# Edge attention on a graph: the scans of a step read PSUM in place, and k and q of a turn share one PSUM tile of two banks

## The chip, the cores and the metric

The kernel runs on one core of a Trainium2 chip. The metric is the time of one execution in device microseconds; several runs give a median. A profile is taken of one more execution.

## The reference

A pre-norm attention layer on a graph of 12,500 nodes with 128 features and 212,500 edges, 8 heads of 16. The edges come sorted by destination, and every node has an edge to itself.

```python
h = jnp.maximum(_layernorm(x, axis=-1), 0.0)
# in the layer, node_h is h
q = (node_h @ Wq.T + bq).reshape(N, NUM_HEADS, HEAD_DIM)
k = (edge_h @ Wk.T + bk).reshape(-1, NUM_HEADS, HEAD_DIM)
v = (node_h @ Wv.T + bv).reshape(N, NUM_HEADS, HEAD_DIM)
qs, qd = (q[src], q[dst])
in_m = jnp.sum(qs * k, axis=-1)
out_m = jnp.sum(qd * k, axis=-1)
diag_m = jnp.sum(qs * qd, axis=-1)
score = (_segment_softmax(in_m * SCALE, dst, N) + _segment_softmax(out_m * SCALE, dst, N)
         + _segment_softmax(diag_m * SCALE, dst, N)) * att
h = jax.ops.segment_sum(score[..., None] * v[dst], dst, num_segments=N)
out = h @ Wo.T + bo        # reshaped to 128 features; then leaky_relu, and x is added
```

Every edge thus needs three products of 128 features (q of its source, q of its destination, k of the edge), summed by head to 24 logits. Each of the 24 columns goes through a softmax over the edges of one destination; its maximum over a destination's run of edges is found with scans.

## The kernel before

There are two paths in the file; with edges sorted by destination `ordered_path` runs. A head part makes the table of q for all nodes in memory (`q_table`). Then comes the loop that takes most of the time: 83 steps t (G = 83) of 5 turns s (S = 5), g = 5t + s, 415 turns in all. A turn is 512 edges, as 4 groups of 128 (BE = 512, JN = 4). A tail brings the last steps and the output of the last nodes.

The order on every engine is written out by hand: `pin` ties each instruction to the one before it on its engine. Engines wait for each other by semaphores that the framework puts in from the tiles that instructions share. Each turn issues, in this order:

- `turn(g+2)`: TensorE transposes the edge features (4 transposes into `eT_ps`, one PSUM bank), ScalarE copies them to `eT`.
- `spread_q(g+1)`: 4 matmuls of a one-hot matrix with a window of q rows (`win`) bring q of the destinations into `qd_ps`; ScalarE copies it to `qd` (L1268), because VectorE needs it also as the partner of k, which lies in PSUM.
- `project(g+1)`: a bias matmul (L1255) and 8 matmul records of fp32 (L1257) make k in `k_ps`.
- `logits(g)`: VectorE multiplies q of the sources with q of the destinations (L1276), with k (L1277), and `qd` with k (L1278), then sums by head (L1279).
- `one_hots(g+3)`: ScalarE makes the one-hot matrix of a later turn (L698, L699).

POOL (GpSimd) gathers q of the sources, 4 indirect DMAs a turn, 26 turns ahead (L707). Each is made to wait for a product instruction of TensorE, so that it is issued close behind it: the first for the transposes of the turn, the second for the q matmuls, the third for the k matmuls, the fourth for the last one of the turn:

```python
turn(g + 2);     behind[g + 1, 0] = pinned[products]
spread_q(g + 1); behind[g + 1, 1] = pinned[products]
project(g + 1);  behind[g + 1, 2] = pinned[products]
...
behind[g + 1, 3] = pinned[products]
```

Beside this, each step does once what the softmax of two steps earlier needs. At s = 4, `turn_logits(t-1)` transposes the logits to 120 rows (5 turns x 24 columns) by 512 edges, `l_ps`, and at s = 0 `turn_head(t-1)` transposes the first 64 edges of them, `h_ps`: a run of edges may go on into the next block, so a scan needs up to 64 logits beyond its end. ScalarE copies both into one tile `u` of 576 (L1304, L1318). At s = 1, `scan_both(t-2)` makes a forward and a backward maximum scan over the 576 with `far` (0 within a run, far below between runs). At s = 2, `turn_max` transposes the maxima to `m_ps`, and `powers` subtracts (VectorE, L1389) and takes the exponential (ScalarE, L1390). At s = 3, `show_ends` makes a matrix that selects the window of destinations (`d_ps`, then ScalarE L1425, L1426), and `weigh_powers` multiplies with the edge weights (L1408). At s = 4, `to_rows` sums into rows of destinations (`w_ps`, L1436; ScalarE L1441), which `put_rows` sends to memory. Output nodes are made in between (`nodes_before`, `nodes_between`). The small PSUM tiles of these steps share three buffers.

Of the kernel before, what the change touches and what calls it, by code (L numbers as in the profile page):

```python
# [7 lines left out]
F32 = mybir.dt.float32  # L8
BF = mybir.dt.bfloat16
I32 = mybir.dt.int32  # L10
AF = mybir.ActivationFunctionType
ALU = mybir.AluOpType
# [9 lines left out]
FAR = 1e30  # L22
# [450 lines left out]
def ordered_path(ctx: ExitStack, tc: tile.TileContext, flag, x, src, dst, edge_attr, edge_weight,  # L473
# [19 lines left out]
    nc = tc.nc  # L493
# [7 lines left out]
    S = 5  # L501
# [149 lines left out]
    def fetch(t):  # L651
# [5 lines left out]
        if t < G:  # L657
            relb = load.tile([K3, S, BE], BF, name="relb")
            pin(nc.sync.dma_start(relb, rel_d[part].rearrange("(s b) e -> s b e", b=G)
                                  [None, :, at, :].to_broadcast([K3, S, BE])))  # L660
        n = (BE + HEAD if t < G - 2 else BE) + 1
        far = load.tile([R, BE + HEAD + 1], BF, name="far", bufs=4)
        lo = t * BE
        of = bass.AP(far_d.tensor, far_d.offset + lo, [[G * BE, S], [0, H3], [1, n]])
        pin(nc.sync.dma_start(far[:, :n], of))
        to = [mybir.EngineType.SP] if t < G else [mybir.EngineType.SP, mybir.EngineType.Activation]
# [573 lines left out]
    with tc.tile_pool(name="work", bufs=2) as work, \  # L1240
            tc.tile_pool(name="scan", bufs=2) as scan, \
            tc.tile_pool(name="ps", bufs=1, space=PSUM) as ps:
        ks, eTs, qds, q_ps, lTs = {}, {}, {}, {}, {}

        def turn(g):
            eT_ps = ps.tile([P, JN, P], F32, name="eT_ps", bufs=1)
            for j in range(JN):
                pin(nc.tensor.transpose(eT_ps[:, j, :], eas[g][:, j * F:(j + 1) * F], ident))  # L1248
            eT = work.tile([P, JN, P], F32, name="eT", bufs=2)
            pin(nc.scalar.copy(eT, eT_ps))  # L1250
            eTs[g] = eT

        def project(g):
            k_ps = ks[g] = ps.tile([P, JN, F], F32, name="k_ps", bufs=2)
            pin(nc.tensor.matmul(k_ps, ones3, bk3, start=True, stop=False))  # L1255
            for j in range(JN):
                pin(nc.tensor.matmul(k_ps[:, j, :], eTs[g][:, j, :], wk, start=False,  # L1257
                                     stop=(j == JN - 1)))
            del eTs[g]

        def spread_q(g):
            s, d = g % S, st[g // S]
            qd_ps = q_ps[g] = ps.tile([P, JN, F], F32, name="qd_ps", bufs=2)
            for j in range(JN):
# [6 lines left out]
        def logits(g):  # L1271
            s, t = g % S, g // S
            if s == 0:
                lTs[t] = scan.tile([P, JN, S, H3], F32, name="lT", bufs=4)
            prod = work.tile([P, JN, 3, F], F32, name="prod", bufs=1)
            pin(nc.vector.tensor_mul(prod[:, :, 1, :], qqs[g], q_ps[g]))  # L1276
            pin(nc.vector.tensor_mul(prod[:, :, 0, :], qqs[g], ks[g]))  # L1277
            pin(nc.vector.tensor_mul(prod[:, :, 2, :], qds[g], ks[g]))  # L1278
            pin(nc.vector.tensor_reduce(lTs[t][:, :, s, :],  # L1279
                                        prod.rearrange("p j i (h d) -> p j (i h) d", d=DIM), AX.X,  # L1280
                                        ALU.add))
            del ks[g], qds[g], q_ps[g], qqs[g]

# [12 lines left out]
        def turn_logits(t):  # L1296
            l_ps = small([R, P, JN], "l_ps")
            for j in range(JN):
                pin(nc.tensor.transpose(l_ps[:, :, j], lTs[t][:, j].rearrange("p s c -> p (s c)"),  # L1299
                                        ident))  # L1300
            l = st[t]["l"] = l_ps.rearrange("r p j -> r (p j)")
            if t < G - 2:
                u = st[t]["u"] = scan.tile([R, BE + HEAD], F32, name="u")
                pin(nc.scalar.copy(u[:, :BE], l))  # L1304

        def turn_head(t):
            n = HEAD // JN
            h_ps = small([R, n, JN], "h_ps")
            for j in range(JN):
                pin(nc.tensor.transpose(h_ps[:, :, j], lTs[t][:n, j].rearrange("p s c -> p (s c)"),  # L1310
                                        ident[:n, :n]))
            head = h_ps.rearrange("r p j -> r (p j)")
            if t == 0:
                l_few = scan.tile([R, HEAD], F32, name="l_few", bufs=1)
                pin(nc.scalar.copy(l_few, head))
                pin(nc.sync.dma_start(l_end[:R - H3, :], l_few[H3:, :]))
            else:
                pin(nc.scalar.copy(st[t - 1]["u"][:, BE:], head))  # L1318

# [20 lines left out]

        def scan_both(t):
            d = st[t]
            u, far = d["u"], d["far"]
            pin(nc.vector.tensor_tensor_scan(u, far[:, :BE + HEAD], u, last.get("u", -FAR), op0=ALU.add,
                                             op1=ALU.max))
            last["u"] = u[:, BE - 1:BE]
            m = d["m"] = scan.tile([R, BE + HEAD], F32, name="m")
            pin(nc.vector.tensor_tensor_scan(m[:, ::-1], far[:, BE + HEAD:0:-1], u[:, ::-1], -FAR,
                                             op0=ALU.add, op1=ALU.max))
# [14 lines left out]
        def scan_back(t):  # L1364
            d = st[t]
            if t < G:
                m = d["m"] = scan.tile([R, BE + HEAD], F32, name="m")[:, :BE]
                pin(nc.vector.tensor_tensor_scan(m[:, ::-1], d["far"][:, BE:0:-1], d["u"][:, ::-1],
# [94 lines left out]
        def later(f, t, *more):  # L1463
            if 0 <= t < T:
                f(t, *more)
# [217 lines left out]
        for g in range(end):  # L1683
# [17 lines left out]
            if s == 0:  # L1701
                later(turn_head, t - 1)
                later(select, t - 2)
            elif s == 1:
                later(scan_both, t - 2)
                if t == 3:
                    logits_few()
# [83 lines left out]
        for r, of in enumerate(rest):  # L1791
# [3 lines left out]
            halves_of(ab, engine)  # L1795
        names = ("eT_ps", "k_ps", "qd_ps", "qd_ps", "k_ps")
        for r in range(len(rest) + 2):
            if r < len(rest):
# [4 lines left out]
                of.turn(small([P, JN, P], "node_ps"))  # L1803
                of.project_o(ps.tile([P, JN, F], F32, name=names[r], bufs=1 if r == 0 else 2))
            if 0 <= r - 2:
# [47 lines left out]
```

## Time and profile before

| | |
|---|---|
| median of 3 runs | 2729.59 us (2725.22 to 2730.32) |
| profiled execution | 2736.8 us, span 2735.0 us |
| mean granted TensorE clock | 0.741 |
| TensorE busy | 1955.8 us (72%) |
| VectorE busy | 2035.8 us (74%) |
| ScalarE busy | 1455.5 us (53%) |
| GpSimd busy | 1610.2 us (59%) |
| memory read, written | 322.07 MB, 32.17 MB |

Busy time is that of an engine's own instructions; register, branch, semaphore and DMA-issuing instructions don't count. "PE" is TensorE's matmuls, "PEld" its weight loads, DVE is VectorE, ACT ScalarE, POOL GpSimd, SP the engine that issues most DMAs. In a row of the timeline the columns are the start, the duration, engine, line, operation, tiles and shapes, the number of equal instructions run together, and in brackets the idle time of the engine before it with what ended it; "remote" is a semaphore whose sender the view doesn't name. In a row of a group "| a, b | c" are busy time in all, mean of one in ns, and idle time in front of them.

### The profile page before, as it was taken

What the parts mean: (1) busy time and instruction counts of PE and PEld (TensorE: products, weight loads), DVE (VectorE), ACT (ScalarE), POOL (GpSimd) and SP (SyncE); (2) the same over time, 40 slices, a digit from 0 to 9 for tenths busy, and PEclk for the clock granted to TensorE, in tenths of its full rate; (3) what the DMA queues carried; (4) which work ended last, traced back from release to release, by engine and by line L of the source; (5) the groups of instructions that cost most, each with busy time, mean ns of one, the idle gap of its engine ahead of it and who ended that gap; (6) DMA issues with size and microseconds to landing.
All of it is one profiled execution on the core that took longest, in us unless ns stands there. A gap on an engine that the chain in (4) does not pass through costs nothing.

```text
span 2735.0 us, 37777 instructions
## 1 busy us (share of the span) xinstructions
PE 1955.8 (72%) x10956; PEld 1537.5 (56%) x10956; DVE 2035.8 (74%) x2644; ACT 1455.5 (53%) x2824; POOL 1610.2 (59%) x1683
## 2 busy tenths in 40 slices
PE   2366776776677777777777877777768777777886
PEld 1245665555555555555555655565556566555664
DVE  2265777777778777787777777787777777777995
ACT  1355765555555555555555555555555555555672
POOL 7516566666666666666666666666666666666100
PEclk9977777667777777776677677667777676768785
DMA  6256344554554455444444444444444544554431
GB/s 177 76 166 190 111 130 121 142 145 124 136 145 130 139 147 138 139 136 137 128 129 140 123 130 131 134 120 131 134 127 120 139 135 122 134 134 123 123 85 51
DMA packets 378949, 356.98 MB, mean 131 GB/s; under 512 B 192899, under 2 KB 298638, under 8 KB 378528
## 3 DMA queue, kind: packets, MB, share of 16 engines
q1 hardware_dynamic: 310109, 239.36, 30.4%
q0 software_dynamic: 53184, 108.92, 15.5%
q10 hardware_dynamic: 15440, 6.20, 0.9%
q8 instruction: 90, 1.47, 0.2%
q14 instruction: 126, 1.02, 0.1%
HBM read 322.07 MB, written 32.17 MB: 130 GB/s over the span
## 4 chain that ended last, share of the span: by engine, by line
PE 52%; issue 13%; ACT 13%; DVE 10%; another core or an unknown queue 9%; DMA 1%; SPq 0%; POOL 0%; ACTq 0%; DVEq 0%; POOLq 0%
PE k_ps L1257 14%; PE eT_ps L1248 8%; PE w_ps L1436 7%; PE qd_ps L1265 5%; PE k_ps L1255 4%; PE node_ps L1187 2%; PE m_ps L1380 2%; DVE lT L1279 2%; PE d_ps L1422 2%; ACT qd L1268 2%; ACT relb L698 2%; ACT eT L1250 2%; PE l_ps L1299 2%; ACT oh L699 1%
## 5 line engine op out<-in xcount | busy, mean ns | idle before, releaser
L707 POOL DMA_INDIRECT qq<-q_table,sources x1564 | 1503.5, 961 | 893.7 <-issue 339.7
L1279 DVE TENSOR_REDUCE lT<-prod 128x96 f32<-128x1536 f32 x415 | 727.5, 1753 | 14.3
L1257 PE MATMUL k_ps<-wk,eT 128*128 128x128 f32 x3320 | 637.6, 349 | 19.2 <-issue 18.4
L1257 PEld LDWEIGHTS k_ps<-wk,eT 128*128 128x128 f32 x3320 | 539.0, 246 | 156.9 <-issue 155.7
L1248 PE MATMUL eT_ps<-ident,ea 128*128 128x128 f32 x1660 | 352.4, 349 | 272.9 <-issue 161.7
L1248 PEld LDWEIGHTS eT_ps<-ident,ea 128*128 128x128 f32 x1660 | 249.1, 179 | 356.5 <-issue 210.3
L1276 DVE TENSOR_TENSOR prod<-qq,qd_ps 128x512 f32<-128x512 f32 x412 | 280.3, 680 | 192.1 <-ACT qd L1268 98.4
L1277 DVE TENSOR_TENSOR prod<-qq,k_ps 128x512 f32<-128x512 f32 x412 | 280.7, 681 | 185.6 <-remote 100.7
L1268 ACT COPY qd<-qd_ps 128x512 f32<-128x512 f32 x415 | 245.7, 592 | 254.4 <-PE qd_ps L1265 96.2
L1250 ACT COPY eT<-eT_ps 128x512 f32<-128x512 f32 x415 | 241.5, 582 | 253.5 <-remote 105.6
L1436 PE MATMUL w_ps<-back,sel 128*126 128x144 f32 (+1 forms) x1296 | 223.4, 347 | 122.7 <-ACT sel L1426 103.1
L698 ACT ACTIVATE relb<-relb,before 126x512 bf16<-126x512 bf16 x415 | 303.9, 732 | 0.0
L1436 PEld LDWEIGHTS w_ps<-back,sel 128*126 128x126 f32 (+1 forms) x1296 | 213.0, 241 | 134.1 <-ACT sel L1426 111.7
L1278 DVE TENSOR_TENSOR prod<-qd,k_ps 128x512 f32<-128x512 f32 x415 | 281.8, 679 | 0.0
L699 ACT ACTIVATE oh<-relb 126x512 bf16<-126x512 bf16 x415 | 261.3, 630 | 13.2
L1265 PE MATMUL qd_ps<-win,oh 126*128 126x128 bf16 x1660 | 209.6, 261 | 13.0 <-issue 12.8
L1255 PE MATMUL k_ps<-b,ones 3*128 3x512 bf16 x415 | 198.4, 478 | 4.1 <-issue 2.4
L1265 PEld LDWEIGHTS <-oh 126*128 126x128 bf16 x1660 | 167.8, 122 | 28.2 <-issue 13.3
L1390 ACT ACTIVATE back<-back 128x480 f32<-128x480 f32 x83 | 50.0, 603 | 186.4 <-DVE back L1389 119.4
L1380 PE MATMUL m_ps<-ident,m 120*128 120x120 f32 x332 | 72.1, 347 | 97.9 <-issue 70.5
L1389 DVE TENSOR_TENSOR back<-lT,m_ps 128x480 f32<-128x480 f32 x83 | 54.0, 650 | 112.6 <-PE d_ps L1422 71.6
L1425 ACT ACTIVATE sel<-d_ps 128x420 f32<-128x420 f32 x168 | 77.8, 512 | 94.4 <-remote 84.5
(232 smaller groups left out, 1955.8 us busy)
## 6 DMA issues: line engine op xcount, KB each, us to landing
ea<-in_edge_attr_dram SPq DMA_DIRECT2D x415, 256.0 KB
relb<-rel_d SPq DMA_DIRECT2D x83, 630.0 KB
qq<-q_table,sources POOLq DMA_INDIRECT x1564
win<-q_table SPq DMA_DIRECT2D x415, 31.5 KB
far<-far_d SPq DMA_DIRECT2D x81, 135.2 KB
q_table<-q SPq DMA_DIRECT2D x24, 384.0 KB
sums<-rows SPq DMA_DIRECT2D x411, 7.9 KB
q_table<-xq SPq DMA_DIRECT2D x24, 256.0 KB
```

Source lines behind the costliest of these rows:

```text
L698: pin(nc.scalar.activation(d, d, AF.Abs, bias=before[:K3]))
L699: pin(nc.scalar.activation(oh, d, AF.Relu, bias=1.0, scale=-1.0))
L707: rows = pin(nc.gpsimd.indirect_dma_start(out=qq[:, j, :], out_offset=None, in_=x if g < RAW else q_table, in_offset=bass.IndirectOffsetOn ...
L1248: pin(nc.tensor.transpose(eT_ps[:, j, :], eas[g][:, j * F:(j + 1) * F], ident))
L1250: pin(nc.scalar.copy(eT, eT_ps))
L1255: pin(nc.tensor.matmul(k_ps, ones3, bk3, start=True, stop=False))
L1257: pin(nc.tensor.matmul(k_ps[:, j, :], eTs[g][:, j, :], wk, start=False, stop=(j == JN - 1)))
L1265: pin(nc.tensor.matmul(qd_ps[:, j, :], ohs[g][:, j * P:(j + 1) * P], d["win"][:, s, :], start=(j == 0), stop=(j == JN - 1)))
L1268: pin(nc.scalar.copy(qds[g], qd_ps))
L1278: pin(nc.vector.tensor_mul(prod[:, :, 2, :], qds[g], ks[g]))
L1279: pin(nc.vector.tensor_reduce(lTs[t][:, :, s, :], prod.rearrange("p j i (h d) -> p j (i h) d", d=DIM), AX.X, ALU.add))
L1436: pin(nc.tensor.matmul(w_ps[:(hi - lo) * W, lo:hi].rearrange("p s c -> p (s c)"), d["sel"][:n, j, lo:hi, :].rearrange("p s w -> p (s w)"), ...
```

## The change

k and q of a turn get one PSUM tile of two banks, `qk_ps`. The products of q of the sources with q of the destinations and with k become one VectorE instruction of 128x1024; the product of `qd` with k stays. The tile `eT` gets a third buffer. ScalarE's copies into `u` are dropped: the forward scan of a step runs in place in `l_ps` at s = 0 (`scan_here`), and copies its last column to a carry tile of 120x1; the 64 columns beyond the end have two scans of their own, one forward from `h_ps` and one backward (`scan_head`, at s = 0), and the backward scan over the 512 starts from their result (`scan_back`, which the tail had, at s = 1). `far` is 513 wide instead of 577. `logits_few`, which runs once, moves from t = 3 to t = 1, and the end of the kernel takes its PSUM tiles from the new ones. Lines shift by up to 9.

```diff
--- before.py
+++ after.py
@@ -658,11 +658,10 @@
             relb = load.tile([K3, S, BE], BF, name="relb")
             pin(nc.sync.dma_start(relb, rel_d[part].rearrange("(s b) e -> s b e", b=G)
                                   [None, :, at, :].to_broadcast([K3, S, BE])))
-        n = (BE + HEAD if t < G - 2 else BE) + 1
-        far = load.tile([R, BE + HEAD + 1], BF, name="far", bufs=4)
+        far = load.tile([R, BE + 1], BF, name="far", bufs=4)
         lo = t * BE
-        of = bass.AP(far_d.tensor, far_d.offset + lo, [[G * BE, S], [0, H3], [1, n]])
-        pin(nc.sync.dma_start(far[:, :n], of))
+        of = bass.AP(far_d.tensor, far_d.offset + lo, [[G * BE, S], [0, H3], [1, BE + 1]])
+        pin(nc.sync.dma_start(far, of))
         to = [mybir.EngineType.SP] if t < G else [mybir.EngineType.SP, mybir.EngineType.Activation]
         loads, base_v[t] = nc.values_load_multi_w_load_instructions(
             places[0:1, t, 0:S], engines=to, min_val=0, max_val=N - 1,
@@ -1240,18 +1239,18 @@
     with tc.tile_pool(name="work", bufs=2) as work, \
             tc.tile_pool(name="scan", bufs=2) as scan, \
             tc.tile_pool(name="ps", bufs=1, space=PSUM) as ps:
-        ks, eTs, qds, q_ps, lTs = {}, {}, {}, {}, {}
+        qks, eTs, qds, lTs = {}, {}, {}, {}
 
         def turn(g):
             eT_ps = ps.tile([P, JN, P], F32, name="eT_ps", bufs=1)
             for j in range(JN):
                 pin(nc.tensor.transpose(eT_ps[:, j, :], eas[g][:, j * F:(j + 1) * F], ident))
-            eT = work.tile([P, JN, P], F32, name="eT", bufs=2)
+            eT = work.tile([P, JN, P], F32, name="eT", bufs=3)
             pin(nc.scalar.copy(eT, eT_ps))
             eTs[g] = eT
 
         def project(g):
-            k_ps = ks[g] = ps.tile([P, JN, F], F32, name="k_ps", bufs=2)
+            k_ps = qks[g][:, 0]
             pin(nc.tensor.matmul(k_ps, ones3, bk3, start=True, stop=False))
             for j in range(JN):
                 pin(nc.tensor.matmul(k_ps[:, j, :], eTs[g][:, j, :], wk, start=False,
@@ -1260,7 +1259,8 @@
 
         def spread_q(g):
             s, d = g % S, st[g // S]
-            qd_ps = q_ps[g] = ps.tile([P, JN, F], F32, name="qd_ps", bufs=2)
+            qks[g] = ps.tile([P, 2, JN, F], F32, name="qk_ps", bufs=2)
+            qd_ps = qks[g][:, 1]
             for j in range(JN):
                 pin(nc.tensor.matmul(qd_ps[:, j, :], ohs[g][:, j * P:(j + 1) * P],
                                      d["win"][:, s, :], start=(j == 0), stop=(j == JN - 1)))
@@ -1273,13 +1273,13 @@
             if s == 0:
                 lTs[t] = scan.tile([P, JN, S, H3], F32, name="lT", bufs=4)
             prod = work.tile([P, JN, 3, F], F32, name="prod", bufs=1)
-            pin(nc.vector.tensor_mul(prod[:, :, 1, :], qqs[g], q_ps[g]))
-            pin(nc.vector.tensor_mul(prod[:, :, 0, :], qqs[g], ks[g]))
-            pin(nc.vector.tensor_mul(prod[:, :, 2, :], qds[g], ks[g]))
+            pin(nc.vector.tensor_mul(prod[:, :, 0:2, :].rearrange("p j i f -> p i j f"),
+                                     qqs[g][:, None].to_broadcast([P, 2, JN, F]), qks[g]))
+            pin(nc.vector.tensor_mul(prod[:, :, 2, :], qds[g], qks[g][:, 0]))
             pin(nc.vector.tensor_reduce(lTs[t][:, :, s, :],
                                         prod.rearrange("p j i (h d) -> p j (i h) d", d=DIM), AX.X,
                                         ALU.add))
-            del ks[g], qds[g], q_ps[g], qqs[g]
+            del qks[g], qds[g], qqs[g]
 
         last = {}
         assert len(rest) <= REST
@@ -1298,10 +1298,7 @@
             for j in range(JN):
                 pin(nc.tensor.transpose(l_ps[:, :, j], lTs[t][:, j].rearrange("p s c -> p (s c)"),
                                         ident))
-            l = st[t]["l"] = l_ps.rearrange("r p j -> r (p j)")
-            if t < G - 2:
-                u = st[t]["u"] = scan.tile([R, BE + HEAD], F32, name="u")
-                pin(nc.scalar.copy(u[:, :BE], l))
+            st[t]["l"] = l_ps.rearrange("r p j -> r (p j)")
 
         def turn_head(t):
             n = HEAD // JN
@@ -1309,13 +1306,11 @@
             for j in range(JN):
                 pin(nc.tensor.transpose(h_ps[:, :, j], lTs[t][:n, j].rearrange("p s c -> p (s c)"),
                                         ident[:n, :n]))
-            head = h_ps.rearrange("r p j -> r (p j)")
+            st[t]["l_head"] = h_ps.rearrange("r p j -> r (p j)")
             if t == 0:
                 l_few = scan.tile([R, HEAD], F32, name="l_few", bufs=1)
-                pin(nc.scalar.copy(l_few, head))
+                pin(nc.scalar.copy(l_few, st[t]["l_head"]))
                 pin(nc.sync.dma_start(l_end[:R - H3, :], l_few[H3:, :]))
-            else:
-                pin(nc.scalar.copy(st[t - 1]["u"][:, BE:], head))
 
         def logits_few():
             eT_ps = small([P, EL], "few_ps")
@@ -1338,14 +1333,21 @@
             pin(nc.scalar.copy(lT, l_ps))
             pin(nc.sync.dma_start(l_end[R - H3:, :EL], lT))
 
-        def scan_both(t):
+        def scan_here(t):
             d = st[t]
-            u, far = d["u"], d["far"]
-            pin(nc.vector.tensor_tensor_scan(u, far[:, :BE + HEAD], u, last.get("u", -FAR), op0=ALU.add,
+            u = d["u"] = d["l"]
+            pin(nc.vector.tensor_tensor_scan(u, d["far"][:, :BE], u, last.get("u", -FAR), op0=ALU.add,
                                              op1=ALU.max))
-            last["u"] = u[:, BE - 1:BE]
-            m = d["m"] = scan.tile([R, BE + HEAD], F32, name="m")
-            pin(nc.vector.tensor_tensor_scan(m[:, ::-1], far[:, BE + HEAD:0:-1], u[:, ::-1], -FAR,
+            last["u"] = scan.tile([R, 1], F32, name="carry")
+            pin(nc.vector.tensor_copy(last["u"], u[:, BE - 1:]))
+
+        def scan_head(t):
+            far = st[t]["far"]
+            u = scan.tile([R, HEAD], F32, name="u_head")
+            pin(nc.vector.tensor_tensor_scan(u, far[:, :HEAD], st[t]["l_head"], last["u"], op0=ALU.add,
+                                             op1=ALU.max))
+            head = st[t - 1]["head"] = scan.tile([R, HEAD], F32, name="head")
+            pin(nc.vector.tensor_tensor_scan(head[:, ::-1], far[:, HEAD:0:-1], u[:, ::-1], -FAR,
                                              op0=ALU.add, op1=ALU.max))
 
         def scan_on(t):
@@ -1364,7 +1366,7 @@
         def scan_back(t):
             d = st[t]
             if t < G:
-                m = d["m"] = scan.tile([R, BE + HEAD], F32, name="m")[:, :BE]
+                m = d["m"] = scan.tile([R, BE], F32, name="m")
                 pin(nc.vector.tensor_tensor_scan(m[:, ::-1], d["far"][:, BE:0:-1], d["u"][:, ::-1],
                                                  d["head"][:, 0:1], op0=ALU.add, op1=ALU.max))
             else:
@@ -1700,10 +1702,13 @@
             one_hots(g + 3)
             if s == 0:
                 later(turn_head, t - 1)
+                later(scan_here, t - 2)
+                if t > 1:
+                    scan_head(t - 1)
                 later(select, t - 2)
             elif s == 1:
-                later(scan_both, t - 2)
-                if t == 3:
+                later(scan_back, t - 2)
+                if t == 1:
                     logits_few()
             elif s == 2:
                 later(turn_max, t - 2)
@@ -1793,7 +1798,10 @@
             if of.more is not None:
                 pin(engine.tensor_add(ab, ab, of.more))
             halves_of(ab, engine)
-        names = ("eT_ps", "k_ps", "qd_ps", "qd_ps", "k_ps")
+        places_o = [ps.tile([P, JN, F], F32, name="eT_ps", bufs=1)]
+        for r in range(2):
+            qk_ps = ps.tile([P, 2, JN, F], F32, name="qk_ps", bufs=2)
+            places_o += [qk_ps[:, 0], qk_ps[:, 1]]
         for r in range(len(rest) + 2):
             if r < len(rest):
                 of = rest[r]
@@ -1801,7 +1809,7 @@
                 scores_of(ends_ab[:, r * JN:r * JN + of.n], of.score[:, :of.n])
                 of.weigh(of.held)
                 of.turn(small([P, JN, P], "node_ps"))
-                of.project_o(ps.tile([P, JN, F], F32, name=names[r], bufs=1 if r == 0 else 2))
+                of.project_o(places_o[r])
             if 0 <= r - 2:
                 rest[r - 2].add_x(nc.vector)
                 rest[r - 2].store()
```

## The prediction, made before the changed kernel ran

> **What bounds the kernel now.** First the page's busy line and chain.
>
> ```profile
> span 2735.0 us, 37777 instructions
> PE 1955.8 (72%) x10956; PEld 1537.5 (56%) x10956; DVE 2035.8 (74%) x2644; ACT 1455.5 (53%) x2824; POOL 1610.2 (59%) x1683
> PE 52%; issue 13%; ACT 13%; DVE 10%; another core or an unknown queue 9%; DMA 1%; SPq 0%; POOL 0%; ACTq 0%; DVEq 0%; POOLq 0%
> ```
>
> No engine is full, and the chain changes engine all the time: the engines wait for one another. The span is 2735.0 us of a profiled execution of 2736.8 (1.8 us lie around it), 7 us above the median of 2729.59; I sum against the profile and take 7 off at the end. Next, the loop of 83 steps of 5 turns by the windows view (sum, PE, PEld, DVE, ACT, POOL, granted clock, DMA share, GB/s), and two windows of one step.
>
> ```profile
> 206.00:2660.00 2454.00, 1824.56 (x10285) 1441.66 (x10286) 1909.48 (x2251) 1356.01 (x2598) 1509.38 (x1572) 0.73 0.48 132
> 1411.00:1421.00 10.00, 8.85 (x36) 6.31 (x36) 8.30 (x10) 5.13 (x9) 7.55 (x8) 0.53 0.63 185
> 1431.00:1441.00 10.00, 6.48 (x50) 5.08 (x49) 7.57 (x9) 5.04 (x11) 6.48 (x8) 0.99 0.65 162
> ```
>
> A step takes 2454/83 = 29.57 us (5.91 a turn). In it PE works 21.98 us, VectorE 23.0, ScalarE 16.3, and POOL 18.2 on 18.9 gathers. The clock is 0.53 in one window and 0.99 in another; with it PE's work per turn changes.
>
> Then the timeline inside a step, which shows what the averages don't.
>
> ```profile
> 1402.27 0.39 PE L1265 MATMUL qd_ps<-win,oh 126*128 126x128 bf16 x4
> 1402.59 0.38 PE L1255 MATMUL k_ps<-b,ones 3*128 3x512 bf16 x1
> ...
> 1406.68 0.59 ACT L1268 COPY qd<-qd_ps 128x512 f32<-128x512 f32 x1 [2.35 <-PE qd_ps L1265]
> ...
> 1408.38 1.03 POOL L707 DMA_INDIRECT qq<-q_table,sources  x1 [0.30 <-issue]
> ...
> 1408.72 0.74 PE L1380 MATMUL m_ps<-ident,m 120*128 120x120 f32 x4 [1.01 <-issue]
> ...
> 1411.04 0.69 DVE L1277 TENSOR_TENSOR prod<-qq,k_ps 128x512 f32<-128x512 f32 x1 [1.80 <-remote]
> 1411.09 0.58 ACT L1250 COPY eT<-eT_ps 128x512 f32<-128x512 f32 x1 [2.54 <-remote]
> 1411.27 0.94 POOL L707 DMA_INDIRECT qq<-q_table,sources  x1 [1.86 <-remote]
> ...
> 1411.58 0.59 ACT L1268 COPY qd<-qd_ps 128x512 f32<-128x512 f32 x1
> ...
> 1411.73 1.12 PE L1248 MATMUL eT_ps<-ident,ea 128*128 128x128 f32 x4 [2.27 <-ACT eT L1250]
> ```
>
> PE finished q at 1402.66 and began k at once; ScalarE's copy of that q began only at 1406.68, 4.0 us later. All three consumers at 1411 start together, 1.63 to 1.86 us after POOL's gather ended at 1409.41, though PE had done their inputs long before. So, as I read it, news of PE's work reaches the others late while POOL issues gathers, and comes soon after POOL falls idle. That POOL is the cause is an inference; the late arrival is in the rows. In the tail, where POOL no longer gathers, it is prompt:
>
> ```profile
> 2649.73 0.60 PE L1299 MATMUL l_ps<-ident,lT 128*120 128x128 f32 x4
> ...
> 2650.37 0.58 ACT L1304 COPY u<-l_ps 120x512 f32<-120x512 f32 x1
> ```
>
> Here 0.04 us pass. The loop therefore breathes: POOL gathers, runs out of permission (its gathers are tied behind PE's products), falls idle, the news arrives, all go on. The gathers' own pace is 0.94 busy + 0.30 issue; by the window row 18.9 x (0.96 + 0.30) = 23.9 us of a step. The remaining 5.7 us are idle gaps: at 1.86 us each (the POOL row above), 3.1 gaps a step.
>
> **The change part by part.** *VectorE's products.* Rows of the page and of one scan:
>
> ```profile
> L1276 DVE TENSOR_TENSOR prod<-qq,qd_ps 128x512 f32<-128x512 f32 x412 | 280.3, 680 | 192.1 <-ACT qd L1268 98.4
> L1277 DVE TENSOR_TENSOR prod<-qq,k_ps 128x512 f32<-128x512 f32 x412 | 280.7, 681 | 185.6 <-remote 100.7
> L1279 DVE TENSOR_REDUCE lT<-prod 128x96 f32<-128x1536 f32 x415 | 727.5, 1753 | 14.3
> L1344 DVE TENSOR_TENSOR_SCAN u<-far,u 120x576 f32<-120x576 bf16 x81 | 114.6, 1415 | 0.0
> L1348 DVE TENSOR_TENSOR_SCAN m<-far,u 120x576 f32<-120x576 bf16 x81 | 109.9, 1357 | 2.8
> L1356 DVE TENSOR_TENSOR_SCAN qq<-far,u,l_ps x1: 1274/1274/1274, 2664.4 to 2664.4; 120x512 f32<-120x512 bf16 x1
> L1356 DVE TENSOR_TENSOR_SCAN qq<-far,qq,l_end x1: 326/326/326, 2683.0 to 2683.0; 120x64 f32<-120x64 bf16 x1
> L1361 DVE TENSOR_TENSOR_SCAN head<-far,qq x2: 291/291/291, 2681.5 to 2683.4; 120x64 f32<-120x64 bf16 x2
> L1368 DVE TENSOR_TENSOR_SCAN m<-far,head,qq x2: 1284/1284/1284, 2681.8 to 2683.7; 120x512 f32<-120x512 bf16 x2
> ```
>
> Two products of 128x512 (1.36 us) become one of 128x1024, which no row shows. The nearest longer instruction, the reduction of 1536, gives (1753 - 680)/1024 = 1.05 ns an element, so 680 + 512 x 1.05 = 1.22 us and 0.14 saved a turn. Below, a second bank could cost all of it: 0. I take 0.1 a turn, 0.5 a step, with 0 to 0.7 as ends. Against it stands that the part with q can't run any more while k is awaited: up to 0.6 us later after each such wait, on an engine with idle time. [...] *The scans.* Out: 1.415 + 1.357 = 2.77 us a step. In: 1.274 + 1.284 + 0.326 + 0.291 = 3.18, plus the carry copy of 120x1, which has no row (0.1 to 0.3, the 64-wide scan being above it): 3.3 to 3.5. VectorE's net is -0.2 (0.5 - 0.7) to +0.7 us a step (0.7 - 0); I take +0.2, 17 us over the loop if it all showed. VectorE has 29.57 - 23.0 = 6.6 us of idle time a step that covers it; without that cover it costs these 17.
>
> *ScalarE's copies into u.*
>
> ```profile
> L1304 ACT COPY u<-l_ps 120x512 f32<-120x512 f32 x81 | 47.6, 588 | 44.3 <-PE qd_ps L1265 17.5 <-PE h_ps L1310 11.5 <-PE eT_ps L1248 8.1
> L1318 ACT COPY u<-h_ps 120x64 f32<-120x64 f32 x81 | 16.1, 198 | 34.0 <-remote 13.8 <-PE node_ps L1179 10.7 <-PE k_ps L1257 6.0
> ```
>
> 63.7 us of work and 78.3 of waiting in front of it go. ScalarE works 55% of the loop, and the waits return as waits for the next PE product, so I count 0 to 0.79 us a step (the busy part) and take 0. The carry, the shorter far tile on SP's queue (64 columns fewer), the third eT buffer and the scans' place (turns 0 and 1 instead of 1) cost nothing: m is wanted in turn 2 as before, and the turn between covers it. l_ps and h_ps stay in their pool of three PSUM buffers until the scans have read them, but the next to need l_ps's buffer comes after m_ps, which waits for those scans anyway.
>
> *The shared tile.* This is the term that decides. In the changed program k and q of a turn are one tile of two banks, and its waits go by the tile: the bias matmul that opens k (now L1254) waits for ScalarE's copy of the same turn's q (L1268). Before, k's wait was VectorE's product of two turns earlier, long met. Behind the waiting matmul in PE's order stand k's eight matmuls, the next transposes and the next q; VectorE's products wait for k, POOL's third gather too. So PE may no longer run ahead of ScalarE: every turn, PE writes q, the news crosses, ScalarE does eT and q (starts 0.49 apart, 1411.09 and 1411.58), the news comes back, PE goes on. In the rows k of the turn at 1402 would begin not at 1402.59 but after 1407.27; the one after it would wait for the copy that ends at 1412.17.
>
> Two workings for a step. (a) POOL: five crossings a step at which PE's products stand, hence five gaps and not 3.1. At 1.86 us a gap: 23.9 + 9.3 = 33.2 us, +3.6, x 83 = +299. (b) PE: 21.98 us of work, five times the two copies and a crossing half way between 0.04 and 1.86 (0.49 + 0.59 + 0.95 = 2.03): 32.1 us, +212, before any other wait of PE. The waits that remain at s = 2 have a row:
>
> ```profile
> ACT back L1390 <- DVE back L1389: 119.4, 38, 6.1
> ```
>
> 119.4/83 = 1.44 us a step, during which ScalarE holds the q copy behind its exp; now PE would stand behind it as well: 33.6 us, +332. I take (a), +299, between the two; VectorE's +0.2 lies under it. Low end: one of the five crossings is hidden by a gap that is there anyway, 31.3 us, +147. High end: (a) with the exp wait on top, 34.6, +421.
>
> **Rivals.** *Crossings stay as long as now* (worse). From the end of q to the end of its copy the rows give 4.6 us (1402.66 to 1407.27). If PE stood 3.0 us of it every turn beside its 4.40 of work, a turn takes 7.4, a step 37.0: +617, 3347 us. For it: late news is in the rows. Against: with PE standing, POOL's bursts shorten to four gathers (5.0 us), and the news comes when it stops. The main case has a stand of 33.2/5 - 4.40 = 2.2 us; from about 2.6, half way, this one decides. Half clock belongs to it:
>
> ```profile
> 1409.40:1411.80 2.40, 0.13 (x2) 0.07 (x2) 0.76 (x2) 0.71 (x2) 0.54 (x2) 0.66 0.21 50
> 1411.80:1413.80 2.00, 2.00 (x10) 1.31 (x10) 1.97 (x2) 1.61 (x3) 1.39 (x3) 0.50 0.96 330
> ```
>
> Behind a PE gap of about 2.3 us the clock is 0.50. [...]
>
> *The wait is hidden* (mild): ScalarE, freed of the u copies, keeps up with PE, and only VectorE's trade is left, with a product that waits for both q and k: +0.2 to +0.7 us a step, +37 in the middle, 2767 us. Against: 4.0 us of delay in the rows.
>
> *Lockstep is faster* (other side): what delays the news is POOL's long burst. If PE halts each turn, bursts are cut to four gathers, and the news could cross in 0.04 to 0.9 us; the eT transposes need no stand of their own any more, as ScalarE copies eT ahead of q. Then a gap costs less than the threshold (29.57 - 23.9)/5 = 1.13 us; below that the kernel gains. At 0.9 us: 28.4 us a step, -97, 2633 us. For: the tail's 0.04 us. Against: the three starts at 1411, which needed 1.63 to 1.86 us even after POOL had stopped.
>
> *It doesn't do what it says*: the dependency could turn out met early and the products save nothing: 2725 to 2735.
>
> **How the numbers follow.** A measurement of this kernel can tell 0.2%, some 5.5 us. Main case, PE standing for the q copy: chance 0.52, 2736.8 + 299 - 7 = 3029, I write 3030; its own range 2875 to 3150. Long crossings: 0.16, 3347. Hidden: 0.10, 2767. No change: 0.04. Faster: 0.18, 2633. Faster by over 0.2%: 0.18; within: 0.04; slower: 0.78. The range goes from 2670 (leaving out most of the faster case, about 0.11) to 3350 (leaving out half of the longest, 0.08).
>
> **What would show it.** Right: idle time before the bias matmul (L1254), put down to ScalarE's qd copy, 1 to 2 us x 415; POOL with five gaps a step and its bursts four gathers long; more half clock than a mean of 0.73; the new product near 1.2 us. Wrong: no idle time before L1254, or shorter gaps than 1.1 us with the step below 29.6; then the crossing is not what I think it is. If VectorE's busy time falls by over 1 us a step, its terms are mis-sized.

## The result, and the profile after

The changed kernel takes 3076.09 us (median of 6 runs, 3048.38 to 3090.33) where the kernel before takes 2727.4: ratio 1.1267 (1.1238 to 1.1296). Forecast were 3030 us, and slower. One thing is needed to read the rest: the kernel before took 2727 us on the chip of this result, 2763 on that of the first four experiments and 2206 to 2208 on the three chips of the later eight, so only ratios to the kernel before on the same chip, or differences on one chip, are compared. Those three agree so closely that they are called the quick chip below.

The page of the changed kernel, its busy line and the groups that moved (in a group: busy time in all, mean in ns, idle time in front of it):

```profile
span 3075.7 us, 37396 instructions
PE 1979.6 (64%) x10956; PEld 1606.0 (52%) x10956; DVE 2047.5 (67%) x2472; ACT 1423.0 (46%) x2662; POOL 1588.1 (52%) x1683
L706 POOL DMA_INDIRECT qq<-q_table,sources x1564 | 1481.9, 947 | 1214.0 <-issue 329.7
L1276 DVE TENSOR_TENSOR prod<-qq,qk_ps 128x1024 f32<-128x1024 f32 x412 | 501.7, 1218 | 514.0 <-PE qk_ps L1256 340.0
L1254 PE MATMUL qk_ps<-b,ones 3*128 3x512 bf16 x415 | 199.9, 482 | 947.0 <-ACT qd L1268 633.2
L1249 ACT COPY eT<-eT_ps 128x512 f32<-128x512 f32 x415 | 241.4, 582 | 491.5 <-remote 280.8
```

TensorE stood 947.0 us before the bias matmul that opens k (this idle time is the stand below, and a crossing is the time from the end of a product to the start of what waits for it); before the change that row had 4.1. The idle time in front of the eT transposes fell from 272.9 us to 4.0: in all 413 turns that have both, ScalarE's eT copy was done before the q copy that TensorE now waits for. POOL's idle time went from 893.7 to 1214.0: in the loop it now pauses for over 0.5 us between gathers 5.7 times a step and not 3.4 times, at about 1.75 us each in both. Each of the four engines is busy within 2.3% of its time before, and all wait more. The windows view of the loop (columns as in the prediction):

```profile
202.00:3003.00 2801.00, 1850.18 (x10308) 1513.68 (x10308) 1929.27 (x2087) 1327.92 (x2446) 1487.17 (x1572) 0.72 0.42 116
```

A step takes 2801/83 = 33.7 us instead of 29.6. In the timeline of a step:

```profile
1416.68 0.39 PE L1265 MATMUL qk_ps<-win,oh 126*128 126x128 bf16 x4
1416.88 0.94 POOL L706 DMA_INDIRECT qq<-q_table,sources  x1 [0.30 <-issue]
...
1418.61 0.94 POOL L706 DMA_INDIRECT qq<-q_table,sources  x1 [0.79 <-PE qk_ps L1265]
...
1420.52 0.59 ACT L1249 COPY eT<-eT_ps 128x512 f32<-128x512 f32 x1 [4.83 <-remote]
1420.76 0.94 POOL L706 DMA_INDIRECT qq<-q_table,sources  x1 [1.21 <-remote]
...
1421.01 0.59 ACT L1268 COPY qd<-qk_ps 128x512 f32<-128x512 f32 x1
...
1421.65 0.58 PE L1254 MATMUL qk_ps<-b,ones 3*128 3x512 bf16 x1 [4.58 <-ACT qd L1268]
```

q is ready at 1417.07; ScalarE, idle for 4.83 us, hears of its two inputs at 1420.52, and TensorE goes on at 1421.65. But the turns aren't alike. Sorting the 415 idle times before L1254 by their turn in the step gives means of 1.34, 1.05, 4.44, 1.03 and 3.55 us for k of turns 0 to 4: two of the five hold 70% of the stand. The long one of turn 2, in the rows above, is late news; from when the transposes are done and ScalarE is free, it starts the eT copy ahead of that stand 3.37 us later (median), those of the other four turns 0.00 to 0.04 us later.

### The profile page after: what moved, and what is told of

It is laid out like the page before. It is cut to its first block, busy times and chain, and to the rows that moved or that the text cites. A ratio compares the mean times of both kernels' runs of the same rounds, so it can differ in the third digit from the quotient of the medians.

```text
span 3075.7 us, 37396 instructions
## 1 busy us (share of the span) xinstructions
PE 1979.6 (64%) x10956; PEld 1606.0 (52%) x10956; DVE 2047.5 (67%) x2472; ACT 1423.0 (46%) x2662; POOL 1588.1 (52%) x1683
## 4 chain that ended last, share of the span: by engine, by line
PE 44%; issue 17%; ACT 16%; another core or an unknown queue 13%; DVE 6%; DMA 2%; POOL 1%; SPq 0%; DVEq 0%; ACTq 0%; POOLq 0%
PE qk_ps L1256 17%; PE w_ps L1438 6%; ACT qd L1268 5%; PE qk_ps L1254 5%; PE eT_ps L1247 4%; PE node_ps L1186 2%; ACT eT L1249 2%; DVE prod L1276 2%; DVE lT L1279 2%; PE d_ps L1424 2%; ACT relb L697 1%; ACT oh L698 1%; POOL qq L706 1%; ACT sel L1427 1%
## 5 line engine op out<-in xcount | busy, mean ns | idle before, releaser
L706 POOL DMA_INDIRECT qq<-q_table,sources x1564 | 1481.9, 947 | 1214.0 <-issue 329.7
L1256 PEld LDWEIGHTS qk_ps<-wk,eT 128*128 128x128 f32 x3320 | 595.0, 269 | 1108.3 <-issue 1108.3
L1276 DVE TENSOR_TENSOR prod<-qq,qk_ps 128x1024 f32<-128x1024 f32 x412 | 501.7, 1218 | 514.0 <-PE qk_ps L1256 340.0
L1254 PE MATMUL qk_ps<-b,ones 3*128 3x512 bf16 x415 | 199.9, 482 | 947.0 <-ACT qd L1268 633.2
L1256 PE MATMUL qk_ps<-wk,eT 128*128 128x128 f32 x3320 | 700.0, 376 | 0.1
L1268 ACT COPY qd<-qk_ps 128x512 f32<-128x512 f32 x415 | 244.5, 589 | 170.0 <-remote 160.9
L1278 DVE TENSOR_TENSOR prod<-qd,qk_ps 128x512 f32<-128x512 f32 x415 | 282.0, 680 | 0.0
L1265 PE MATMUL qk_ps<-win,oh 126*128 126x128 bf16 x1660 | 196.6, 252 | 0.0
L1443 ACT COPY rows<-w_ps 126x144 f32<-126x144 f32 (+1 forms) x162 | 33.5, 258 | 313.2 <-PE w_ps L1438 304.4
L1347 DVE TENSOR_TENSOR_SCAN u_head<-far,carry,h_ps 120x64 f32<-120x64 bf16 x81 | 28.1, 347 | 173.0 <-PE qk_ps L1265 85.7
```

What stands on the lines that cost most here:

```text
L706: rows = pin(nc.gpsimd.indirect_dma_start(out=qq[:, j, :], out_offset=None, in_=x if g < RAW else q_table, in_offset=bass.IndirectOffsetOn ...
L1265: pin(nc.tensor.matmul(qd_ps[:, j, :], ohs[g][:, j * P:(j + 1) * P], d["win"][:, s, :], start=(j == 0), stop=(j == JN - 1)))
L1268: pin(nc.scalar.copy(qds[g], qd_ps))
L1276: pin(nc.vector.tensor_mul(prod[:, :, 0:2, :].rearrange("p j i f -> p i j f"), qqs[g][:, None].to_broadcast([P, 2, JN, F]), qks[g]))
```

## The experiments

**One at a time, beside a kernel before of 2763 us.** First the wait alone:

```diff
 # kernel before
-            pin(nc.scalar.copy(qds[g], qd_ps))
+            copied[g] = pin(nc.scalar.copy(qds[g], qd_ps)).ins.name
...
-            pin(nc.tensor.matmul(k_ps, ones3, bk3, start=True, stop=False))
+            first = pin(nc.tensor.matmul(k_ps, ones3, bk3, start=True, stop=False))
+            tc.add_manual_dep(first.ins, copied[g], ...)
```

> The kernel before with one wait more and nothing else: the bias matmul of k is made to wait for ScalarE's copy of the same turn's q. Two tiles, three products and the scans stay. Theory: the whole loss, 3020 to 3130 us. Rival (the wait by itself is hidden, since other work covers it, and the loss needs the combined product): 2730 to 2850.

3108.33 us, ratio 1.1267 (1.1245 to 1.1288): the ratio of the whole change, with two tiles, three products and the old scans. The changed kernel itself was not run on this chip, and on the quick chip its ratio is another, so the agreement to the last digit is chance; the next run is its counterpart here.

```profile
L1255 PE MATMUL k_ps<-b,ones 3*128 3x512 bf16 x415 | 206.4, 497 | 979.3 <-ACT qd L1271 726.5
```

Then only the shared tile and its product in the kernel before, nothing of the scans:

```diff
 # kernel before
-            k_ps = ks[g] = ps.tile([P, JN, F], F32, name="k_ps", bufs=2)
+            k_ps = qks[g][:, 0]
...
-            qd_ps = q_ps[g] = ps.tile([P, JN, F], F32, name="qd_ps", bufs=2)
+            qks[g] = ps.tile([P, 2, JN, F], F32, name="qk_ps", bufs=2)
+            qd_ps = qks[g][:, 1]
...
-            pin(nc.vector.tensor_mul(prod[:, :, 1, :], qqs[g], q_ps[g]))
-            pin(nc.vector.tensor_mul(prod[:, :, 0, :], qqs[g], ks[g]))
+            pin(nc.vector.tensor_mul(prod[:, :, 0:2, :].rearrange("p j i f -> p i j f"),
+                                     qqs[g][:, None].to_broadcast([P, 2, JN, F]), qks[g]))
...
```

> The kernel before with only the shared tile and the product of 128x1024; the copies into u, the two scans of 576 and two eT buffers stay. Theory: nearly the whole loss, 3020 to 3130 us (the u copies sit in front of the q copy in ScalarE's order at two turns of a step, so it may be above the changed kernel). Rival (the scans carry a good part of the loss): 2730 to 2900.

3106.17 us, ratio 1.1269 (1.1212 to 1.1325): with the wait that comes along, the shared tile and its product cost what the wait alone does. And the changed kernel with this same diff taken back (two tiles, three products; scans in PSUM, narrow far and three eT buffers kept):

> The changed kernel with q and k in a tile of one bank each and three products of 128x512 again; the scans in PSUM, the narrow far tile and the third eT buffer stay. Theory: the loss is gone, and what stays is the trade of the scans, VectorE +0.5 to 0.8 us a step against ScalarE's dropped copies: 2710 to 2780 us. Rival (the scans in PSUM cost, as VectorE holds l_ps and waits for h_ps at turn 0): 2850 or more.

2762.58 us, ratio 1.0000 (0.9986 to 1.0014). Last, the change with only the order of k and q turned round, the tile now being claimed in `project`:

```diff
 # changed kernel
-                spread_q(g + 1)
-                behind[g + 1, 1] = pinned[products]
                 project(g + 1)
+                behind[g + 1, 1] = pinned[products]
+                spread_q(g + 1)
                 behind[g + 1, 2] = pinned[products]
...
```

> The changed kernel with one thing turned round: in each turn TensorE makes k first and then q of the destinations (the shared tile is claimed by k). The bias matmul of k then waits for VectorE's last product of two turns earlier, not for ScalarE's copy of the same turn's q; the single product of 128x1024, the scans in PSUM and the tile of two banks all stay. Theory (the wait of k for the q copy is the whole loss): 2720 to 2780 us, idle time of TensorE before the bias matmul from 947 us to under 50. Rival (the loss lies in the combined product, which needs both k and q before it can start, or in the scans): 3000 to 3080, as the changed kernel.

2765.52 us, ratio 1.0011 (1.0000 to 1.0022), and the stand is gone:

```profile
L1255 PE MATMUL qk_ps<-b,ones 3*128 3x512 bf16 x415 | 198.9, 479 | 37.2 <-issue 18.9 <-DVE prod L1278 11.5 <-DVE prod L1276 6.7
```

With k first, its bias matmul waits for VectorE's product of two turns earlier, and no engine reads the tile until both halves are written. So on this chip the wait that the shared tile brings, in this order of k and q, is the whole loss; scans, far tile and wide product come to nothing together.

**How old the wait is.** The wait of the first experiment, on the copy one turn older, on the quick chip:

```diff
 # kernel with the wait alone
-            tc.add_manual_dep(first.ins, copied[g], ...)
+            tc.add_manual_dep(first.ins, copied[max(g - 1, 0)], ...)
```

> The kernel before with the same extra wait as in the one-wait kernel, but a turn older: the bias matmul of k waits for ScalarE's copy of the previous turn's q. Theory (the loss is the missing turn of slack, not the wait as such): ratio 0.995 to 1.02, since the transposes wait for a copy of that age already. Rival (any wait of k for ScalarE costs, by its own handling): ratio over 1.05.

2207.66 us, ratio 0.9992 (0.9973 to 1.0010). A turn of slack hides it all. (The younger wait by itself was not run on this chip; the changed kernel, which has it, costs 1.1558 there, as shown below.)

**Do the gathers make the news late?** Both kernels without the gathers of turns 29 to 414:

```diff
     def gather(g):
         if g < end:
+            if g >= LOOK + FIRST:
+                qqs[g] = firsts[0]
+                return
```

> The kernel before without the gathers of turns 29 to 414: VectorE multiplies with one tile that stays in place, so those logits are not the reference's. POOL then has nothing to issue in the loop. Theory (news of TensorE's work is late because POOL issues gathers): the median delay from the end of q's matmuls to the start of ScalarE's copy falls under 1 us, and a step is set by VectorE's 23.0 us of work: 23 to 25 us, 2190 to 2360 us in all. Rival (the delay belongs to the semaphores or to ScalarE's order): 2600 or more.

> The changed kernel, again without the gathers of turns 29 to 414 (same omission). TensorE still waits every turn for the copy of q. Theory: with prompt news the stand is the two copies and little else, some 1.2 us a turn, on a TensorE that has room: 0 to 150 us above the same omission in the kernel before. Rival (the wait costs about the same whatever POOL does): 300 us or more above it.

These ran on the quick chip, where the kernel before, gathers and all, needs 2208.14 us. Without them it needs 2140.00, ratio 0.969 (0.9655 to 0.9724), below the forecast. The median delay from q to ScalarE's copy is 0.85 us, under 1 as foreseen; but the kernel with the older wait, gathers and all, has 0.85 on that chip too, so this pair can't say what POOL does to late news. The changed kernel without them needs 2539.91, 400 us above that: the rival's outcome. The cost of the wait doesn't need POOL's gathers, nor late news. The waits of the changed kernel without gathers point to where it comes from; the last row is ScalarE's exponential, held by VectorE's difference:

```profile
PE qk_ps L1257 <- ACT qd L1271: 637.7, 415, 4.3
ACT rows L1446 <- PE w_ps L1441: 323.8, 81, 4.6
ACT back L1395 <- DVE back L1394: 290.2, 83, 4.7
```

**The exponential in front of the copy.** The changed kernel again, and the same with ScalarE's exponential of turn 2 issued at the end of turn 3:

```diff
 # changed kernel, powers(t), for t < G - 2
-                pin(nc.scalar.activation(e, e, AF.Exp, scale=SCALE))
 # turn 3, ahead of show_ends
+                later(raise_e, t - 2)    # the same activation
```

> The changed kernel as it is, on the chip of this call, as a base for the two beside it. If the chip is one on which the kernel before needs some 2210 us, theory (TensorE's stand costs by ScalarE's order, whatever the crossing): ratio 1.15 to 1.20, as without the gathers; rival (on such a chip the stand is short and hidden): 1.00 to 1.06. On a chip with 2730 to 2760 it is 1.127 again.

> The changed kernel with one instruction of ScalarE moved: the exponential of a step is issued at the end of turn 3 instead of turn 2, so that the copies of eT and q of the turn between don't stand behind a VectorE result. Theory (one turn in five has a stand of 3.5 to 4.4 us because the q copy is queued behind the exponential): that stand falls to the 1.0 us of the others, 2.4 to 3.4 us a step, 150 to 280 us under the changed kernel. Rival (the long stand belongs to late news, not to the exponential): within 60 us of the changed kernel.

The changed kernel: 2551.72 us, ratio 1.1558 (1.1525 to 1.1590). With the exponential later: 2237.80, ratio 1.0125 (1.0102 to 1.0148). One moved instruction a step brings back 314 of 343 us, somewhat more than foreseen. Timeline of the changed kernel on the quick chip, where the exponential stands in front:

```profile
1205.50 0.38 PE L1265 MATMUL qk_ps<-win,oh 126*128 126x128 bf16 x4 [0.53 <-DMA relb<-rel_d]
...
1207.15 0.65 DVE L1391 TENSOR_TENSOR back<-lT,m_ps 128x480 f32<-128x480 f32 x1
...
1207.83 0.60 ACT L1392 ACTIVATE back<-back 128x480 f32<-128x480 f32 x1 [4.73 <-DVE back L1391]
...
1208.34 0.57 ACT L1249 COPY eT<-eT_ps 128x512 f32<-128x512 f32 x1
...
1208.81 0.59 ACT L1268 COPY qd<-qk_ps 128x512 f32<-128x512 f32 x1
...
1209.45 0.58 PE L1254 MATMUL qk_ps<-b,ones 3*128 3x512 bf16 x1 [3.56 <-ACT qd L1268]
```

q is ready at 1205.88, but ScalarE, in the order written for it, is at the exponential, which waits for VectorE's difference, which stands behind a whole turn's products; TensorE stands 3.56 us, and with it the k that VectorE wants next. The same place with the exponential later:

```profile
1203.96 1.06 PE L1247 MATMUL eT_ps<-ident,ea 128*128 128x128 f32 x4
...
1204.70 0.94 POOL L706 DMA_INDIRECT qq<-q_table,sources  x1 [0.30 <-issue]
...
1204.84 0.61 PE L1265 MATMUL qk_ps<-win,oh 126*128 126x128 bf16 x4
1205.06 0.58 ACT L1249 COPY eT<-eT_ps 128x512 f32<-128x512 f32 x1 [1.85 <-PE eT_ps L1247]
...
1205.54 0.59 ACT L1268 COPY qd<-qk_ps 128x512 f32<-128x512 f32 x1
...
1206.19 0.58 PE L1254 MATMUL qk_ps<-b,ones 3*128 3x512 bf16 x1 [0.73 <-ACT qd L1268]
```

The stand is 0.73. For the whole run, the row of the view of waits and the busy line of the page, first with the exponential in front, then with it later:

```profile
PE qk_ps L1254 <- ACT qd L1268: 636.7, 415, 4.3
PE 1814.9 (71%) x10956; PEld 1464.2 (57%) x10956; DVE 2032.6 (80%) x2472; ACT 1406.3 (55%) x2662; POOL 1597.7 (63%) x1683
```

```profile
PE qk_ps L1254 <- ACT qd L1268: 427.4, 410, 3.0
PE 1630.1 (73%) x10956; PEld 1308.7 (59%) x10956; DVE 2022.9 (90%) x2472; ACT 1411.0 (63%) x2662; POOL 1592.0 (71%) x1683
```

TensorE still stands 427 us, about 1.0 us a turn, with VectorE 90% busy beside it: those stands hide almost wholly (2237.80 us beside 2208.37 of the kernel before), and the one of 3.5 us a step is the loss. Its removal took 209 us off the stands and 314 off the time. The mean granted clock rose from 0.788 to 0.879, and the same matmuls took 185 us less, which may be where the other 105 come from; no run parts the two. The kernel with the older wait has the exponential in the same place, and ScalarE waits even longer there (row below); but no product of the same turn stands behind its copies, and in an order of that kind moving the exponential gained nothing (the last attempt below):

```profile
ACT back L1393 <- DVE back L1392: 502.9, 82, 8.5
```

**Attempts at a version that beats both**, all on the quick chip. Two PSUM banks for eT_ps, two instead of three for the small tiles, in the kernel before:

```diff
-            eT_ps = ps.tile([P, JN, P], F32, name="eT_ps", bufs=1)
+            eT_ps = ps.tile([P, JN, P], F32, name="eT_ps", bufs=2)
...
-            return ps.tile(shape, F32, name=name, tag="small", bufs=3)
+            return ps.tile(shape, F32, name=name, tag="small", bufs=2)
...
```

> The kernel before with two PSUM banks for eT_ps and two instead of three for the small tiles. Theory (what is left of the waiting is TensorE's round trip with ScalarE): the transposes get a turn more of slack, and the 355 us of idle time before them shrink: ratio 0.96 to 0.99, if the small tiles do with two. Rival (POOL's pace and the late news set the step, or the small tiles then block): 1.00 to 1.03.

2218.93 us, ratio 1.0043 (1.0026 to 1.0060): a miss, in the rival's range. The product of 128x1024 with k first: the kernel before with the diff of the shared tile and that of k before q, the tile claimed in `project`:

> The kernel before with the shared tile and the product of 128x1024, k made before q, and the copies into u and the two scans of 576 as before: the saving of the product without the wait and without the dearer scans. Theory: VectorE does 0.14 us a turn less, 58 us; where VectorE sets the time (the kernel before at some 2210 us, VectorE over 90% busy) the ratio is 0.97 to 0.985, where the crossings set it (2730 to 2760) 0.99 to 1.00. Rival (the product that needs both q and k loses as much as it saves): 1.00 to 1.01 on both.

2222.81 us, ratio 1.0066 (1.0046 to 1.0087): slower, between theory and rival. And the same with the exponential at turn 3, by the diff shown for it:

> The kernel before with the shared tile and its product of 128x1024, k made before q, and the exponential at the end of turn 3; the copies into u and the scans of 576 stay. Theory (what kept the saving of the product back was ScalarE standing behind VectorE's difference at turn 2, 354 us of waiting for the exponential, by which the q copy that the product needs came late): the ratio to before is 0.96 to 0.99 where VectorE sets the time (2210 us), and 0.95 to 1.00 where it doesn't (2730 to 2760). Rival (the product that needs both k and q loses by itself what it saves): 1.00 to 1.01.

2223.09 us, ratio 1.0080 (1.0065 to 1.0096): the theory falls. The busy line, the first product and the gathers, first of the kernel with the older wait (at the time of the kernel before), then of the one with the product and k first:

```profile
PE 1727.9 (78%) x10956; PEld 1367.8 (62%) x10956; DVE 2014.8 (91%) x2644; ACT 1425.6 (65%) x2824; POOL 1635.8 (74%) x1683
L1279 DVE TENSOR_TENSOR prod<-qq,qd_ps 128x512 f32<-128x512 f32 x412 | 279.6, 679 | 73.9 <-DMA qq<-q_table,sources 39.1 <-ACT qd L1271 12.5 <-ACT relb L698 4.7
L707 POOL DMA_INDIRECT qq<-q_table,sources x1564 | 1528.7, 977 | 476.6 <-issue 214.0
```

```profile
PE 1755.2 (79%) x10956; PEld 1367.1 (62%) x10956; DVE 1988.1 (90%) x2229; ACT 1435.2 (65%) x2824; POOL 1644.9 (74%) x1683
L1277 DVE TENSOR_TENSOR prod<-qq,qk_ps 128x1024 f32<-128x1024 f32 x412 | 499.5, 1212 | 106.5 <-DMA qq<-q_table,sources 39.5 <-ACT qd L1269 37.9 <-ACT relb L698 9.0
L707 POOL DMA_INDIRECT qq<-q_table,sources x1564 | 1537.7, 983 | 478.1 <-issue 232.6
```

VectorE's busy time falls by 26.7 us, 0.06 a turn, since neighbouring products overlap: those of 512 last 680 ns but start 598 apart, and the instruction behind the one of 1024 starts 1131 after it, 65 ns less than two of 598. The gain is lost in waiting: 32.6 us of idle time more in front of the product. The rows of POOL, which the theories above left out, say why no attempt could gain. Its gathers follow one another with 0.30 us between (476.6 us over 1564), so it never pauses: gathers and gaps take (1528.7 + 476.6)/83 = 24.2 us a step, more than the 23.0 us of VectorE's work that the prediction counted. On the quick chip POOL thus sets the time of the kernel before, which fits the 68 us that fell with the gathers, when VectorE went to 94% busy. The same sum of gathers and gaps is 10.4, 10.5 and 14.5 us longer in the three attempts, in the order of the text, and they are 10.8, 14.4 and 17.3 us slower. Why a gather takes 982 or 983 ns in them instead of 977 stays open.

## Why the prediction was right

- *The shared tile as the deciding term*: right, and shown. The wait alone gives the whole ratio (1.1267), and taking it away in two ways gives 1.000 and 1.001.
- *Its size*: +299 us was forecast, the median moved by 349; 33.2 us a step against 33.7. Working (a), POOL's gaps, and working (b), TensorE's stand, gave numbers near the truth for a cause that was only partly theirs. The sign of (a) came true: 5.7 pauses a step, where it counted five. But on the quick chip the loss is 400 us without gathers, so there the pauses don't make it; that five equal crossings sum to nearly the right time is in good part luck.
- *Five equal crossings*: wrong. On the chip of the result three turns stand about 1.1 us, one 4.44 and one 3.55. On the quick chip one stands 3.49 and the others 1.00 to 1.15. The term that was mis-sized is the exponential: entered as 1.44 us at the high end only, it alone carried 314 of 343 us on the quick chip. How the 349 us divide between it and the late news on the chip of the result was not tried. By what they stand above the other three's mean of 1.14, turn 2 (late news) has 274 us and turn 4 (by its place, the exponential) 200, together more than 349, so part of them must be hidden.
- *News is late because POOL gathers*: not shown, and not enough as a cause. In the rows above a gather runs from 1204.70 to 1205.64 while news of transposes that end at 1205.02 starts ScalarE at 1205.06. On the chip of the result the same pattern took 3.7 us (transposes done at 1416.84, ScalarE at 1420.52). The traces' records of semaphore updates put the delay at TensorE's end, not at the engines that wait. Of the updates on record for the semaphore that its products raise, all but 3 of 1980 come within 0.06 us of the end of a product in the changed kernel on the quick chip; on the chip of the result 442 of 1703 don't, and before the change 1503 of 1969 didn't, with the same gathers in all three. (Ends of matmuls are modelled, so late work and a late signal can't be told apart.) What makes it late there stays open; no run without gathers fell on such a chip. And the 4.0 us that the prediction read from its rows were not all news: ScalarE was idle for 2.35 of them. The rival "crossings stay as long" was right for one turn in five.
- *Lockstep is faster*: fell, though the short crossings that were its condition came in four turns of five on the chip of the result (the 0.00 to 0.04 us above); the two long stands outweighed them. On the quick chip nearly all crossings are short and the loss is as large, 343 us: there the stand is added to a kernel in which POOL has no pauses to give back and VectorE is 91% busy.
- *VectorE's terms*: the product at 1218 ns (1.22 forecast); its saving 0.06 us a turn on the quick chip and not 0.1, as the sum took durations for spacing. The scans:

```profile
L1339 DVE TENSOR_TENSOR_SCAN l_ps<-far,carry,l_ps x80: 1276/1279/1290, 338.0 to 2977.2; 120x512 f32<-120x512 bf16 x80
L1342 DVE COPY carry<-l_ps x81: 157/157/159, 299.4 to 2978.5; 120x1 f32<-120x1 f32 x81
L1347 DVE TENSOR_TENSOR_SCAN u_head<-far,carry,h_ps x81: 345/347/349, 301.3 to 2981.7; 120x64 f32<-120x64 bf16 x81
L1350 DVE TENSOR_TENSOR_SCAN head<-far,u_head x81: 290/291/292, 301.7 to 2982.1; 120x64 f32<-120x64 bf16 x81
L1370 DVE TENSOR_TENSOR_SCAN m<-far,head,l_ps x81: 1269/1271/1272, 307.0 to 2985.8; 120x512 f32<-120x512 bf16 x81
```

  They sum to 3.35 us a step (3.3 to 3.5 forecast). VectorE's busy time rose by 11.7 us in all (17 were forecast). The scans and the dropped copies cost nothing, as said: ratio 1.0000 with two tiles.
- *More half clock*: hardly so on the chip of the result (0.716 for 0.741). On the quick chip the clock was 0.788 with one stand of 3.5 us a step and 0.879 without it. In the clock record of the changed kernel there (from 210 to 2000 us), none of 212 idle times of TensorE of 0.5 to 1 us that began at full clock has half clock within 2 us of its end, and all 62 of 3 us and more have. In the kernel before on the chip of the result 44 of 45 idle times of 2 to 3 us (counted in the same way) were followed by half clock, which bears out the prediction's reading of its gap of 2.3 us.

## What to carry to other kernels

Here two results shared a tile and the waits went by the whole tile: on the chip of the result TensorE stood 947.0 us in front of k, 633.2 of them put down to the copy of q, and with k first, on the chip of 2763 us, it stood 37.2. So write both before another engine reads either. When a new wait is found, look not at its mean but at what each place in the order queues in front of the releasing instruction; on the quick chip four turns in five bore it almost free (1.00 to 1.15 us of stand each), and one exponential, issued a turn too early, made 314 of the 343 us lost. The VectorE products of 512 lasted 680 ns and started 598 apart, so two of them cost less than their durations say: price a merger by the spacing of the starts. And before an engine's work is shortened, look for one that never pauses: on the quick chip, beside POOL's gathers and gaps of 24.2 us a step, the 26.7 us taken off VectorE's busy time did not show.

## What the runs showed of the hardware

The same kernel took 2727, 2763 and 2206 to 2208 us on different chips; its mean granted clock was 0.741 on the first, 0.72 to 0.75 on the second and 0.76 to 0.81 on the quick chip. In the changed kernel on the chip of the result ScalarE hears of TensorE's transposes 3.7 us after their end in the row quoted; on the quick chip, in the row quoted, after 0.04 us. Where the updates of TensorE's semaphore are on record, they themselves come late on the first chip (442 of 1703 in the changed kernel) and not on the quick one (3 of 1980). Which part of the chip makes this difference was not found.
